# The second turn's order chosen on the chip, and half of the last layer norm run beside the last expert slots

## The chip, the cores and the metric

The kernel runs on one core of one Trainium2 chip. Its time is the device time of one execution in microseconds (us). The engines are named as the profile names them: PE is TensorE (matrix products; PEld are its weight loads), DVE is VectorE, ACT is ScalarE, POOL is GpSimd and SP is SyncE, which here issues DMA transfers and nothing else. Each engine works through its own list of instructions in order.

## The reference

Four sequences ("elements" below) of 1024 rows with 256 features pass an attention layer and then a mixture of experts. Each of the two is followed by adding its input and a layer norm without weights.

```python
x = layernorm(x + attention(x))          # 16 heads, causal, low-rank q, k, v with rotary parts
scores = (x @ router_w + router_b) / max(temperature, 0.1)
gates  = sinkhorn(scores, iters=3)       # per element: rows and columns normalised in turn
vals, idx = top_k(gates, 2)              # two experts of eight for each row
vals  = vals / (sum(vals) + 1e-8)
g = relu(x @ wg[e]);  p = x @ wp[e]      # 256 -> 512
y = (g * p) @ wo[e]                      # 512 -> 256
x = layernorm(x + sum over the two experts of vals * y)
```

4096 rows with two experts each are 8192 pairs of a row and an expert.

## The kernel before

**Attention** is computed element by element. Projections, the layer norm after attention and the router of an element are spread beside the attention of the next one by hand-written budgets (class `Lane`). After the last element's attention come its closing work, its router and the experts.

**Lists.** `route(b)` picks two experts for each row of element b. A matmul with a triangular matrix and one with ones (`so_ps`) count, for each row, how many pairs stand before it in each expert's list, and `base` carries the counts from element to element. Then `scatter` (L846) writes the element's pairs into the list `pairs` in device memory: 16 indirect DMAs, issued by POOL. Each expert owns a region of 4096 + 256 entries in that list. An entry holds the row to read, the row to add to, and the gate. `floor` (used when b is the last but one) lifts each expert's count to at least 512 before the last element is counted, so that the first 512 entries of a region hold pairs of elements 0 to 2 only, or empty ones.

**Slots.** The experts work in slots: a slot takes some consecutive entries of one expert's region.

- First turn: eight slots of 512 entries (`ER`), experts 0 to 7, the entries 0 to 511 of each region. These need nothing of the last element and begin before its router is done.
- Second turn: eight slots of 512 entries, the entries 512 to 1023. It goes through the experts in the order 7, 6, ... 0, and its first slot uses the weights of the first turn's last slot again (`like`).
- Further slots of 256 entries (`SR`), for whatever is left in any region. `lay_out` works out on the chip which expert and which entries each has. Three (`SURE`) always run, with or without entries; if more are needed, the rest run in a conditional block.

In text a slot is called by turn and place: 0_4, 1_7, 2_0. For a slot POOL gathers the rows with indirect DMAs (`gather`, L954, one for each 128 entries, into one of two `xg` buffers). PE transposes them (L993), ACT and DVE split them into a high and a low part (L190, L191), since every fp32 product is taken as three products of fp32r parts (`mm3`, L197 to L199). For each of four pieces of the 512 hidden features PE computes `gp` (gate) and `lp` (linear); ACT applies the relu (L1010), DVE multiplies (L1011), and ACT and DVE split the product (`hh`, `hl`). The output product goes to `eo`; ACT scales it by the gate (L1027) into one of six `eo` buffers, and POOL adds it to `results` in device memory with an indirect DMA that adds (L1028). `results` was filled with the rows x beforehand, so that it ends up as x plus the experts' sum. Two slots may hold the same row, so the adds of a slot wait until those of the slot before have landed (`added`, `after`). SP loads each expert's weights (three times 512 KB), ACT rounds them (L190) and DVE takes the rest (L191).

**The last layer norm** comes when all adds have landed. `results` is taken in eight chunks of 512 rows: SP loads a chunk (L1236), DVE takes mean and variance of its four row blocks (L1250, L1251), POOL works out the inverse deviation and the offset (L1253 to L1257, four small operations), ACT applies them to the first five chunks (L1260) and DVE to the last three (`DZ`, L1268), and SP stores (L1239).

**What sets the order.** The kernel is written with a tile framework: the program's order of calls gives priorities, and a scheduler arranges each engine's instructions by its own estimate of time. That order is fixed when the kernel is built. `hole` and `in_turn` and `apart` are the kernel's own helpers for the order of POOL's indirect transfers and for telling the framework which transfers can't touch the same rows. A tile pool with n buffers for a tag makes the (n+1)-th tile wait until the first one's readers are done: `xg` has two, the statistics `mv` have two, the weights' halves two.

## Time and profile before

| | us |
|---|---|
| median of 13 runs | 1055.88 (1051.23 to 1061.19) |
| profiled execution, its own time | 1054.4 |
| its span in the profile | 1052.7 |
| PE busy | 967.3 (92%) |
| DVE, ACT, POOL busy | 735.9, 624.9, 480.7 |
| first output product of an expert slot to the last output on ACT | 702.4 to 1017.9 |
| last add issued | 1021.25 |
| first load of the last layer norm issued | 1026.60 |
| mean granted clock of PE | 0.972 |

A line of a timeline has the start in us, the duration in us, the engine, the line of the program, the operation, the tile written and those read, the shapes, a count, and in brackets how long the engine stood idle before and what it waited for. `results<-eo,ents` is an indirect add of a slot, `xg<-x_rows,ents` a gather, `pairs<-ent,so_i` a scatter into the list. A line of a table by stretches has the stretch, its length, busy us and number of instructions of PE, PEld, DVE, ACT and POOL, the granted clock of PE (1.00 is full), the mean busy share of the 16 DMA engines, and GB/s. A line of the chain has the start, the duration, and what the end was waiting for then.

### The profile page before, as it was taken

The page shows a single profiled execution, that of the slowest core. Times are in us where ns is not written, and L with a number is a line of the kernel's source. Part 1 is how long each engine was busy: PE and PEld are TensorE (multiplying, and loading weights), DVE is VectorE, ACT ScalarE, POOL GpSimd, SP SyncE. Part 2 cuts the span into 40 slices and gives each one's busy share as a digit, 9 for nine tenths or more (in the row PEclk, how much of TensorE's full clock was granted, in tenths as well). Part 3 has the DMA queues.
Part 4 walks back from the last instruction along what each step waited for, and adds up shares of the span by engine and source line. Part 5 has one row for each costly group of instructions (what it writes and reads, how often), then busy time and mean ns, then how long its engine had stood idle before and what let it go on. Part 6 is the DMA issues. An engine that isn't in the chain of part 4 may idle for free.

```text
span 1052.7 us, 18000 instructions
## 1 busy us (share of the span) xinstructions
PE 967.3 (92%) x6392; PEld 605.1 (57%) x6392; DVE 735.9 (70%) x1630; ACT 624.9 (59%) x1314; POOL 480.7 (46%) x551
## 2 busy tenths in 40 slices
PE   6689999999999999999899999999999999999960
PEld 4455433455544545554345444378888888888960
DVE  3777888888888887788547898284685546555636
ACT  3544666665666666666666676755664546565633
POOL 7176521121451713354323224754477875654535
PEclk9899999999999999999999999989999999999995
DMA  6564421221422403324223330176473765655638
GB/s 242 164 214 139 115 71 56 82 76 47 132 60 67 126 2 122 111 67 122 66 75 97 88 67 3 30 250 149 101 164 94 144 143 123 174 117 137 140 53 319
DMA packets 71362, 119.66 MB, mean 114 GB/s; under 512 B 16416, under 2 KB 43040, under 8 KB 70880
## 3 DMA queue, kind: packets, MB, share of 16 engines
q1 hardware_dynamic: 48544, 81.76, 24.8%
q0 software_dynamic: 20672, 36.41, 15.9%
q8 instruction: 52, 0.85, 0.3%
q10 hardware_dynamic: 2048, 0.27, 0.2%
q14 instruction: 46, 0.38, 0.1%
HBM read 82.52 MB, written 35.60 MB: 112 GB/s over the span
## 4 chain that ended last, share of the span: by engine, by line
PE 73%; DVE 7%; DMA 7%; POOL 4%; ACT 4%; issue 3%; SPq 2%; ACTq 0%; POOLq 0%; DVEq 0%
PE y L437 12%; PE s L353 11%; PE sT L456 10%; PE gp L198 3%; PE gp L199 3%; PE gp L197 3%; PE eo L197 3%; POOL pairs L846 3%; PE eo L199 3%; PE eo L198 3%; PE s L370 2%; PE po L623 2%; PE lp L199 2%; PE lp L198 2%; PE lp L197 2%
## 5 line engine op out<-in xcount | busy, mean ns | idle before, releaser
L462 ACT ACTIVATE pT<-sT 128x512 f32<-128x512 f32 (+1 forms) x608 | 326.4, 576 | 159.1 <-PE sT L456 129.6
L374 DVE TENSOR_REDUCE mx<-s 128x1 f32<-128x384 f32 (+3 forms) x352 | 215.7, 632 | 41.2 <-PE s L370 39.9
L353 PE MATMUL s<-ks,qs 96*128 96x512 bf16 (+3 forms) x768 | 211.8, 330 | 14.5 <-DMA ks<-parts 7.1
L456 PE MATMUL sT<-qs,ks 98*128 98x512 bf16 (+3 forms) x768 | 212.4, 328 | 8.5 <-ACT pT L462 6.7
L474 POOL TENSOR_SCALAR_AFFINE_SELECT pT<-pT 128x512 f32<-128x512 f32 x120 | 75.7, 636 | 268.4 <-ACT pT L462 261.5
L383 DVE TENSOR_REDUCE mx<-s 128x1 f32<-128x512 f32 x256 | 171.2, 681 | 30.8 <-PE s L353 29.8
L437 PE MATMUL y<-pT,va 128*32 128x512 f32 (+3 forms) x1536 | 170.3, 498 | 1.0 <-POOL pT L474 0.6
L1028 POOL DMA_INDIRECT results<-eo,ents x64 | 105.4, 1647 | 81.8 <-ACT eo L1027 67.8
L353 PEld LDWEIGHTS <-qs 96*128 96x128 bf16 x768 | 71.1, 99 | 109.3 <-issue 81.8
L456 PEld LDWEIGHTS <-ks 98*128 98x128 bf16 x768 | 68.8, 99 | 94.1 <-issue 61.3
L370 PE MATMUL s<-mask,ident_b 128*128 128x128 bf16 (+2 forms) x352 | 86.8, 247 | 0.0
L1011 DVE TENSOR_TENSOR relu<-relu,lp 128x512 f32<-128x512 f32 x64 | 43.8, 684 | 61.4 <-ACT relu L1010 37.2
L191 DVE TENSOR_TENSOR wl<-w,wh 128x512 fp32r<-128x512 f32 x108 | 69.6, 684 | 22.1 <-ACT wh L190 20.6
L197 PE MATMUL eo<-wh,hh 128*128 128x256 f32 x280 | 81.6, 293 | 2.6 <-ACT eo L1027 2.1
L198 PE MATMUL eo<-wl,hh 128*128 128x256 f32 x280 | 79.3, 285 | 0.0
L954 POOL DMA_INDIRECT xg<-x_rows,ents x64 | 66.0, 1030 | 27.9 <-issue 16.1
L1010 ACT ACTIVATE relu<-gp 128x512 f32<-128x512 f32 (+1 forms) x76 | 42.7, 563 | 60.6 <-PE gp L199 60.1
L199 PE MATMUL eo<-wh,hl 128*128 128x256 f32 x280 | 78.0, 285 | 0.0
L846 POOL DMA_INDIRECT pairs<-ent,so_i x64 | 64.6, 1010 | 25.2 <-issue 17.5
L191 DVE TENSOR_TENSOR hl<-relu,hh 128x512 fp32r<-128x512 f32 (+1 forms) x76 | 48.4, 646 | 28.4 <-ACT hh L190 27.8
L437 PEld LDWEIGHTS y<-pT,va 128*32 128x32 f32 x1536 | 32.1, 108 | 62.0 <-issue 46.2
L190 ACT CAST wh<-w 128x512 fp32r<-128x512 f32 x108 | 60.7, 620 | 10.3 <-PE gp L198 7.7
(212 smaller groups left out, 1857.9 us busy)
## 6 DMA issues: line engine op xcount, KB each, us to landing
ks<-parts SPq DMA_DIRECT2D x90, 128.0 KB
w<-in_wg_dram SPq DMA_DIRECT2D x18, 512.0 KB
w<-in_wp_dram SPq DMA_DIRECT2D x18, 512.0 KB
w<-in_wo_dram SPq DMA_DIRECT2D x18, 512.0 KB
qs<-parts SPq DMA_DIRECT2D x66, 128.0 KB
parts<-lv POOLq DMA_DIRECT2D x12, 384.0 KB, 3.0
parts<-lv POOLq DMA_DIRECT2D x24, 192.0 KB, 3.2
xh<-in_x_t_dram SPq DMA_DIRECT2D x8, 512.0 KB
```

Source lines behind the costliest of these rows:

```text
L191: (sub or nc.vector).tensor_tensor(lo, src, hi.bitcast(F32), ALU.subtract)
L197: nc.tensor.matmul(ps, lhsT=sh, rhs=mh, start=(i == 0), stop=False)
L198: nc.tensor.matmul(ps, lhsT=sh, rhs=ml, start=False, stop=False)
L199: nc.tensor.matmul(ps, lhsT=sl, rhs=mh, start=False, stop=(i == n - 1))
L353: nc.tensor.matmul(ps, lhsT=q(h, half)[:NROW, t * P : (t + 1) * P], rhs=k(h, kc)[:NROW, :w], start=first, stop=last,)
L370: nc.tensor.matmul(each[:, :, w - P :], lhsT=ident_b, rhs=mask.unsqueeze(1).to_broadcast([P, m, P]), start=False, stop=True,)
L374: nc.vector.tensor_reduce(mx_of[:, half, h0 : h0 + m, t], each, AX.X, ALU.max)
L383: nc.vector.tensor_reduce(mx_of[:, kc, h, t : t + 1], ps, AX.X, ALU.max)
L437: nc.tensor.matmul(acc[g, qc][SLOT * h : SLOT * (h + 1), lo:], lhsT=va[b % 2][:, kb, at : at + SLOT], rhs=pT[:, h, lo:], start=(kb == 0), ...
L456: nc.tensor.matmul(st[:, h % m * w : (h % m + 1) * w], lhsT=k(h, kb // BPQ)[: NROW + 2, kb % BPQ * P : (kb % BPQ + 1) * P], rhs=q(h, qc)[: ...
L462: nc.scalar.activation(pT[:, h + 1 - m : h + 1, lo:], st[:, : m * w].rearrange("p (h t) -> p h t", t=w), AF.Exp, scale=scale,)
L1028: ins = nc.gpsimd.indirect_dma_start(out=results[:, :], out_offset=bass.IndirectOffsetOnAxis(ap=k.ent[:, j, 1:2], axis=0), in_=eo, in_offs ...
```

## The change

It has three parts.

1. `order_of_second`, called in the router of the second element (b = 1), takes the expert that has fewest pairs of the elements 0 and 1, and writes the order of the second turn into a table: it begins with the expert after that one and ends with it. If an expert has over 1024 pairs of these two elements, a number is added to `filled` that makes the conditional block run. The second turn's slots read their expert and their first entry from the table, as the further slots did before: SP loads the values into registers, the entries are loaded slot by slot, and no slot reuses another's weights.
2. The last second slot then holds, if its expert has at most 512 pairs of the elements 0 and 1, nothing that adds to these elements' rows, and nor does any further slot. At the beginning of that slot POOL issues four loads of 512 KB (`load_early`, after the adds of the second turn's last slot but one), which read the rows of the elements 0 and 1 from `results`. Two chunks of them are normed after that slot, one after the first further slot, one after the second (`by_scalar`: statistics on DVE, the four small operations on POOL, application on ACT, store on SP).
3. The last loop takes only the four chunks of the elements 2 and 3, the last two by DVE. In the conditional block, if it runs, the chunks of the elements 0 and 1 are normed again.

Its core ("..." marks what is left out; line numbers are not those of the profile):

```diff
-DZ = 3
+DZ = 2
...
+        if b == EARLY - 1:
+            order_of_second()
...
+    def order_of_second():
+        few = tab("few", [E])
+        nc.vector.tensor_tensor(few, floor[:1], base[:1], ALU.subtract)
+        most, again = tab("most", [1]), tab("again", [1])
+        nc.vector.tensor_reduce(most, few, AX.X, ALU.min)
+        nc.vector.tensor_scalar(again, most, -float(ER), float(NOVER), ALU.is_lt, ALU.mult)
+        tables["again"] = again
+        nc.vector.tensor_reduce(most, few, AX.X, ALU.max)
+        nc.vector.tensor_scalar(few, few, most, None, ALU.is_equal)
...
+        nc.vector.tensor_scalar(seq[:, 0], slot_no[:, :E], most, float(E + 1), ALU.subtract, ALU.add)
+        nc.vector.tensor_copy(seqi[:, 0], seq[:, 0])
+        nc.vector.tensor_single_scalar(seqi[:, 0], seqi[:, 0], E - 1, ALU.bitwise_and)
...
     def pairs_of(k):
-        if k.which == 2:
-            row = value(1, k.s, NLIST - SR)
+        if k.which:
+            row = value(k.table, 1, k.s, NLIST - k.rows)
             k.ent = const.tile([P, k.blocks, 4], I32, name=f"ent_{k.name}")
...
     def weights(k, i):
-        if k.like is not None:
-            return
-        if k.which == 2:
+        if k.which:
             if i == 0:
-                k.e = value(0, k.s, E - 1)
+                k.e = value(k.table, 0, k.s, E - 1)
...
-    def slot(k, between):
+    def slot(k, between, ahead=None):
+        if ahead is not None:
+            ahead()
...
-    second = [Slot(1, e) for e in reversed(range(E))]
-    second[0].like = first[-1]
+    second = [Slot(1, n) for n in range(E)]
...
+    def by_scalar(i, z, name):
+        rstd, off = norm_z(i, z, name)
+        for j in range(BPQ):
+            nc.scalar.activation(
+                z[:, j, :], z[:, j, :], AF.Identity, bias=off[:, j : j + 1], scale=rstd[:, j : j + 1]
+            )
+        store_z(i, z)
...
+    def load_early():
+        for i in range(n_early):
+            z = work.tile([P, T], F32, tag="yT0", name=f"ze{i}", bufs=2) if i < 2 else work.tile(
+                [P, BPQ, C], F32, tag="x1", name=f"ze{i}", bufs=X1_BUFS
+            )
+            z = early_z[i] = z.rearrange("p (n c) -> p n c", c=C) if i < 2 else z
+            ins = nc.gpsimd.dma_start(out=z, in_=rows_of(results, i))
+            for o in added:
+                after(ins, o)
+
+    def run(keys, given=(), ahead={}, behind={}):
         drain(begin(keys, 0, given))
         for n, key in enumerate(keys):
-            slot(key, begin(keys, n + 1, given))
+            slot(key, begin(keys, n + 1, given), ahead.get(n))
+            for i in behind.get(n, ()):
+                by_scalar(i, early_z[i], "e")
 
-    run(first + second + further[:SURE], (0,))
+    keys = first + second + further[:SURE]
+    n = keys.index(second[-1])
+    run(keys, (0,), {n: load_early}, {n: (0, 1), n + 1: (2,), n + 2: range(3, n_early)})
...
-    for i in range(n_z):
-        load_z(i)
-    for i in range(n_z):
+    for i in range(n_early, n_z):
+        zs[i] = zp.tile([P, BPQ, C], F32, tag="z", name=f"z{i}", bufs=n_z - n_early)
+        nc.sync.dma_start(out=zs[i], in_=rows_of(results, i))
+    for i in range(n_early, n_z):
...
         if i < n_z - DZ:
-            for j in range(BPQ):
-                nc.scalar.activation(
-                    z[:, j, :], z[:, j, :], AF.Identity, bias=off[:, j : j + 1], scale=rstd[:, j : j + 1]
-                )
-            store_z(i, z)
+            by_scalar(i, zs[i], "f")
         else:
-            rest.append((i, z, rstd, off))
+            rest.append((i, zs[i], *norm_z(i, zs[i], "f")))
```

`norm_z` holds the statistics and POOL's four operations as the old loop had them. In the second turn's order as built, places are written 1_0 to 1_7; which expert stands at a place is known only on the chip.

## Prediction

> **What bounds the kernel now.** I read first the chain that ended last, then the busy time by stretches, then POOL's, ACT's, DVE's and SP's timelines at the two places that the change touches. The chain's shares:
>
> ```profile
> PE 73%; DVE 7%; DMA 7%; POOL 4%; ACT 4%; issue 3%; SPq 2%; ACTq 0%; POOLq 0%; DVEq 0%
> ```
>
> So TensorE sets the time, and where it doesn't (the end), DMA and DVE do. By stretches (busy us and instructions of each engine, granted clock, DMA share, GB/s):
>
> ```profile
> 800.00:860.00 60.00, 58.27 (x349) 51.14 (x348) 32.36 (x52) 33.23 (x65) 48.49 (x38) 1.00 0.59 124
> 980.00:1000.00 20.00, 19.30 (x149) 18.33 (x148) 13.10 (x26) 13.28 (x32) 10.17 (x7) 1.00 0.60 134
> 1000.00:1020.00 20.00, 16.79 (x139) 16.39 (x137) 8.25 (x20) 9.63 (x25) 7.28 (x5) 1.00 0.34 55
> 1020.00:1040.00 20.00, 0.00 (x0) 0.00 (x0) 9.52 (x48) 6.01 (x12) 9.61 (x20) 0.55 0.75 257
> ```
>
> The reader is to see that PE is all but full up to the last slots, that POOL is the second busiest engine where the turns meet (48.49 of 60), and that from 1020 on PE does nothing: the final layer norm stands alone there. Where the turns meet, POOL's queue:
>
> ```profile
> 791.50 1.00 POOL L846 DMA_INDIRECT pairs<-ent,so_i  x1 [0.30 <-DVE upto L877]
> ...
> 812.32 1.10 POOL L846 DMA_INDIRECT pairs<-ent,so_i  x1 [0.30 <-issue]
> 813.72 1.61 POOL L1028 DMA_INDIRECT results<-eo,ents  x1 [0.31 <-issue]
> 821.22 1.05 POOL L954 DMA_INDIRECT xg<-x_rows,ents  x1 [0.30 <-PE gp L198]
> 825.27 1.43 POOL L954 DMA_INDIRECT xg<-x_rows,ents  x1 [0.30 <-issue]
> ```
>
> Sixteen scatters of the last element's pairs take 791.50 to 813.72; then come four adds, and the gathers of the first second slot (821.22 to 826.7). PE transposes what they bring at 838.18, 7 to 11 us after it lands. The price of the delayed adds shows on ACT, and on PE behind it (the only two PE rows that I take from there):
>
> ```profile
> 817.65 0.47 ACT L1027 ACTIVATE eo<-eo,ents 128x256 f32<-128x256 f32 x1 [5.00 <-DMA results<-eo,ents]
> ...
> 818.17 0.38 PE L197 MATMUL eo<-wh,hh 128*128 128x256 f32 x1 [1.49 <-ACT eo L1027]
> ...
> 838.18 0.60 PE L993 MATMUL xgT_ps<-ident,xg 128*128 128x128 f32 x4
> ```
>
> At the end:
>
> ```profile
> 980.48 1.56 POOL L1028 DMA_INDIRECT results<-eo,ents  x1 [1.01 <-ACT eo L1027]
> 1005.13 0.38 ACT L1010 ACTIVATE relu<-gp 128x256 f32<-128x256 f32 x1 [0.38 <-PE gp L199]
> 1017.40 0.47 ACT L1027 ACTIVATE eo<-eo,ent 128x256 f32<-128x256 f32 x1 [1.78 <-PE eo L199]
> 1014.82 3.82 DMA results<-eo,ent
> 1019.40 6.56 DMA results<-eo,ent
> 1026.60 3.77 SPq L1236 DMA_DIRECT2D z<-results  x8
> 1038.46 1.37 DVE L1250 BATCH_NORM_STATS2 bnst_f<-z 128x6 f32<-128x256 f32 x4
> 1047.31 0.23 POOL L1257 TENSOR_SCALAR off_f<-off_f 128x4 f32<-128x4 f32 x1
> 1047.58 1.38 DVE L1268 TENSOR_SCALAR z<-z,rstd_f,off_f 128x256 f32<-128x256 f32 x4 [0.67 <-POOL off_f L1257]
> ```
>
> An add issued at 1014.82 lands at 1018.64 and POOL's next waiting instruction starts at 1019.40: 4.58 from add to dependent add. From the first z load to the span's end are 1052.7 − 1026.60 = 26.1 us.
>
> **The change, part by part.** Times are of the profiled run, whose own time is 1054.4 (span 1052.7, 1.7 around it); the median is 1055.88, so I add 1.5 at the end.
>
> *Final loop, four chunks instead of eight.* POOL's four little operations a chunk (1.9 us) set the pace. The eighth chunk's last ends at 1047.54; the fourth's would end at 1039.53 with no fifth between. That is 8.0 less; the 1.38 us of DVE, the store and the end behind it stay. Bounds: 4 × 1.57 (DVE's pitch of a chunk, 1036.90 to 1038.46) = 6.3, and 4 × 2.08 (ACT's four norms of a chunk) = 8.3. **−8.0**.
>
> *Adds after the last output.* Before, last ACT scale ends at 1017.87 and the loads go at 1026.60: 8.7. In the built order the last slot's two outputs come as one piece of 24 matmuls, during which the slot's before lands, so only their own adds are left; the least is one add's pitch 1.87 and the row's 3.8 + 1.6 to the load, 7.0. **−1.7** (between −1.7 and 0).
>
> *(a) Where the turns meet.* The order of POOL changes (PE's matmuls that count the lists move too, from 787 to 796.5): after the first turn's last gathers come two adds of the slot then on PE, and only then the sixteen scatters. The second add waits for ACT's scale, which ended at 798.6, so the scatters start at 800.6 instead of 791.50. Sixteen take 22.2 (to 822.8). Then two adds (1.87 each); the next slot's first add waits for their landing: 824.7 + 4.58 = 829.3; four adds to 836.7; then the gathers, four by 1.28, the last issued at 840.6. A gather lands 2.8 to 5.8 us after issue in this trace: 843.4 to 846.4. PE wants the blocks at 838.18. It stands 5.2 to 8.2; the four land one by one, so I take the lower end: **+5.2**. The eo stall of 2.1 us in before (1.49 and the transposes' lateness) is gone, but the gather, not PE's arrival, now decides, so that gains nothing; if gathers came in time, it would give −2.1, which is the lower bound.
>
> *(b) Early norms in the 256-row slots.* The first early load waits for the adds of the last slot but one. Its last add was issued at 980.48; with (a) at 985.7; the built order puts twelve 512-wide matmuls (0.23 us each, 2.8) ahead of its last product: 988.5. Add to dependent 4.58: 993.1. The third of the final loop's loads landed at 1033.64, 7.0 after the first's issue, and issues are about 0.5 to 0.85 apart (0.85 on POOL, rows of x_rows<-x, which landed in 4.3 median): the first lands at 997.4, the fourth about 8.4 after the start, 1001.5. On **DVE** the first statistics stand ahead of the first small slot's first relu product, so all relu work waits for 997.4 + 1.4. From there to the second small slot's first product DVE has four products and four splits (0.41 each), six weight splits (0.63), two xl (0.42), three chunks of statistics (1.57): 12.6. That makes 1011.4. On **POOL** the four adds of the last second slot wait for the early loads (they write what those read): 1002.3 to 1009.8; behind them the second chunk's chain, mixed with the third's, 3.3: 1013.1. On **ACT** the second chunk's norm waits for that, and the third's and fourth's stand behind it, ahead of the second small slot's third and fourth relu: three by 1.55 and 1.4 of its own work, so that the fourth relu comes at 1019.4. In before it was 1005.13, with (a) 1010.3: 9.1 late. After that point the built order leaves PE twelve 256-wide matmuls more than before (0.12 each): 1.4. **+10.5.** Bounds: if POOL's chain came ahead of the adds, only DVE's order would hold (12.6 against 11.84 between the same two products in before, and the first 3 us): about +3; if each further chunk waits for its buffer too (statistics buffers are two) and the loads share with weights at twice the time (+8.4): +18.
>
> *At nothing:* the first second slot now loads its own expert's weights, six ACT casts (0.62) and six DVE subtractions (0.68): ACT and DVE have 33.23 and 32.36 of 60 there; without that cover 4 us. Three 512 KB loads more on SP, which has only loads to issue; the register loads ahead of them delay each by about a microsecond against a slot of 17.9 us of PE. One 32 KB list per slot instead of a common one lands a slot ahead. Thirteen tiny DVE operations for the order run beside the second element's attention; 13 × 0.4 = 5 us if PE waited for them. The four early stores are on SP behind everything that a slot needs.
>
> **Sum:** −8.0 − 1.7 + 5.2 + 10.5 = +6.0. 1054.4 + 6.0 + 1.5 = **1061.9**.
>
> *A rule against it.* The row at 817.65 shows ACT standing 5.00 us for a buffer, with a cast (818.02) and a relu (818.53) behind it that had their inputs. The Trainium skill, "PSUM — Partial Sum Buffer", section Engine vs sequencer instructions, says that the queues of ScalarE, VectorE and GpSimdE are strict FIFO. By it, (b) is paid in full; by the averages of the stretches alone (DVE 13.10, ACT 13.28 of 20) it would be nothing and the sum −4.5. The page "Perfetto Trace Analysis", section Optimization Strategy, speaks for the change: interleaving regimes with different bounds may help.
>
> *Clock.* After an idle 7.1 us early in the trace (41.5 to 48.5) the granted clock is 0.50 for 4 us; after the 1.49 us at 816.7 it stays 1.00. The stall of (a) lies between; in four pieces it is nearer the second, so 0, with +2 at the other end. The page "TensorE: Matmul & The Clock Gate", section What's actually happening, puts the limit at about 3.4 us idle, by which one unbroken stall would pay the 2.
>
> **Rivals.**
> 1. *The norms do hide* (ends faster). DVE and ACT have 7 us of 20 free; if the early loads land before the small slots' relu (that is, by 993), (b) is 1 and the sum −9.7 + 5.2 + 1 = −3.5: 1052.4. It decides from the point where (b) is below 4.5. Against: 980.48 + 4.58 + 4.3 = 989.4 already in before's order, against the product at 988.48.
> 2. *Neither stall:* −9.7 + 0.5: 1046.7. For it: PE's counting matmuls may run as early as before, and the scatters with them. Against: the scatters' 22.2 us on a POOL at 48.49 of 60.
> 3. *Only (b):* the gathers come in time, −9.7 − 2.1 + 10.5 = −1.3 to −9.7 + 10.5 = +0.8: 1054.6 to 1056.7.
> 4. *Transfers collide:* 2 MB read and 2 MB written beside weights where DMA is at 0.60, with a cold clock: (b) 18, (a) 7: +15.3, 1071.2.
> 5. *It doesn't do what it says:* if the chosen expert had over 512 pairs of the first two elements, spare slots would run in addition. The reference's router on these inputs gives 472 to 598, the smallest expert 472, and the further slots needed are three, those that always run; so no.
>
> **How the numbers follow.** Chances: forecast 0.62 (its own range 1057.5 to 1068), rival 1 0.13, 2 0.05, 3 0.08, 4 0.11, 5 0.01. A measurement of this kernel tells 0.2%, 2.1 us. Faster: rivals 1 and 2, 0.18. Same: most of 3, 0.07. Slower: the forecast, 4 and 5, 0.75. Leaving out rival 2 and the far half of 4 gives 1051.5 to 1071.
>
> **What would show it.** Right: gathers of the first second slot issued after 835 and PE idle about 5 us before its transposes; DVE idle before the first early statistics with "DMA ze"; PE busy well under 16 of 20 in the stretches of the small slots; z loads to end about 18 us. Wrong: PE full through the small slots (rival 1), or early loads landing far from 4 to 8 us after issue.

## The result and the profile after

The changed kernel takes **1078.06 us** (median of 10 runs, 1075.31 to 1081.46) against 1055.51 for the kernel before (46 runs): a ratio of 1.0214, 95% interval 1.0198 to 1.0230, or 22.5 us more. The forecast was 1061.9 with a range to 1071.0: the sign was right, the size was not. The profiled execution of after has a span of 1074.4, 21.7 more than the 1052.7 of before, and a time of its own of 1076.1. Six of the eighteen runs below were made, like these, on chips on which the kernel before takes 1056 to 1058 us; the others on chips on which it takes 1102 to 1107 us for another reason (see the last section), so each is told as a ratio to the kernel before on its own chip.

The shares of the chain that ended last, in after:

```profile
PE 70%; DMA 9%; DVE 7%; ACT 5%; POOL 4%; issue 3%; SPq 2%; ACTq 0%; POOLq 0%; DVEq 0%
```

PE has lost 3 points; DMA has 2 more and ACT one. The same stretches as before, in after (busy us and instructions of PE, PEld, DVE, ACT, POOL, then granted clock, DMA share, GB/s):

```profile
800.00:860.00 60.00, 52.64 (x297) 45.22 (x296) 31.43 (x65) 30.42 (x60) 43.76 (x35) 0.94 0.51 115
...
1000.00:1020.00 20.00, 12.98 (x86) 12.37 (x85) 12.27 (x42) 9.70 (x23) 12.05 (x14) 0.83 0.74 238
1020.00:1040.00 20.00, 14.02 (x95) 13.07 (x95) 7.08 (x22) 12.44 (x30) 9.38 (x15) 0.83 0.46 112
1040.00:1060.00 20.00, 6.76 (x51) 5.99 (x49) 3.27 (x9) 3.30 (x8) 6.15 (x4) 0.81 0.41 87
```

PE is no longer full in two places: where the turns meet (52.64 of 60, it was 58.27) and in the small slots (12.98 and 14.02 of 20). In both the granted clock is below 1; in before it was 1.00 in the same stretches up to 1020. No other engine is full over 20 us: DVE and ACT never pass 12.5 of 20 in the small slots. So no engine became the bound; what is missing is time in which the engines wait for each other and for transfers.

To see how much each place costs I lay the two traces' PE lists side by side: PE does the same matmuls in both, so for a moment of before I count the output columns done by then and look up when after has done as many. The difference of the two times is PE's *lag*. What it grows by between two points is what that part of the program lost.

| part | forecast | measured |
|---|---|---|
| to 838 (attention, first turn) | 0 | +0.5 |
| (a) where the turns meet (to 842) | +5.2 | +9.6 |
| second turn (860 to 990) | 0 | +1.4 |
| (b) small slots (990 to 1017) | +10.5 | +18.9 |
| last scale on ACT to the z loads: 7.10, was 8.73 | −1.7 | −1.6 |
| z loads to the end: 18.83, was 26.1 | −8.0 | −7.3 |
| sum | +6.0 | +21.7 |

The rows add up to 21.5; with the lag at the last ACT scale (1048.47 against 1017.87, 30.6) in place of the first four it is 21.7. Both gains came, to 0.1 and 0.7 us. Both losses came in the places named, at nearly twice the size each.

**Where the turns meet.** The timeline of after, POOL's indirect transfers and what PE waited for behind them:

```profile
800.52 1.57 POOL L1052 DMA_INDIRECT results<-eo,ents  x1 [4.24 <-ACT eo L1051]
802.40 1.48 POOL L850 DMA_INDIRECT pairs<-ent,so_i  x1 [0.30 <-issue]
...
825.61 1.60 POOL L1052 DMA_INDIRECT results<-eo,ents  x1 [0.30 <-ACT hh L192]
827.51 1.56 POOL L1052 DMA_INDIRECT results<-eo,ents  x1 [0.30 <-issue]
832.20 1.77 POOL L1052 DMA_INDIRECT results<-eo,ents  x1 [3.13 <-ACT hh L192]
...
839.84 1.00 POOL L981 DMA_INDIRECT xg<-x_rows,ent  x1 [0.30 <-issue]
...
843.68 0.95 POOL L981 DMA_INDIRECT xg<-x_rows,ent  x1 [0.30 <-issue]
842.76 0.30 PE L1015 MATMUL xgT_ps<-ident,xg 128*128 128x128 f32 x1 [3.87 <-DMA xg<-x_rows,ent]
843.95 0.34 PE L1015 MATMUL xgT_ps<-ident,xg 128*128 128x128 f32 x1 [0.90 <-DMA xg<-x_rows,ent]
846.43 0.80 PE L1015 MATMUL xgT_ps<-ident,xg 128*128 128x128 f32 x2 [2.15 <-DMA xg<-x_rows,ent]
```

The reader is to see the forecast order link by link: the second add held back the scatters to 802.40 (in before they began at 791.50), the scatters held back the adds, the add at 827.51 had to land before that at 832.20 (the profile names an ACT cast for this wait; that it was the landing is read from the program, where a slot's adds wait for those of the slot before, and from the distance of 4.69, for 4.58 in before), and the gathers that stood last in the queue went out at 839.84 to 843.68 instead of 821.22 to 825.27. PE stood 3.87, 0.90 and 2.15 us, 6.92 in all. The two stretches of 4 us behind it:

```profile
844.00:848.00 4.00, 1.85 (x8) 1.51 (x9) 0.11 (x1) 0.73 (x2) 3.08 (x4) 0.52 0.40 114
848.00:852.00 4.00, 4.00 (x19) 3.52 (x19) 2.93 (x5) 2.90 (x6) 3.30 (x3) 0.63 0.27 85
```

After the stand the granted clock was 0.52 and then 0.63. Busy time times what is missing of the clock is 1.85 × 0.48 + 4.00 × 0.37 = 2.4 us. 6.9 and 2.4 are the 9.6 but for 0.3.

**The small slots.** The chain of work that ended last in after, where it passes the small slots:

```profile
995.00 8.30 DMA results<-eo,ent
...
1003.91 3.72 DMA ze<-results
1007.65 1.40 DVE bnst_e L1249 x4
```

The same add in POOL's timeline:

```profile
995.00 3.28 POOL L1052 DMA_INDIRECT results<-eo,ent  x1 [1.26 <-ACT eo L1051]
```

The last add of the last slot but one took 8.30 us to land; the median of all adds is 3.9 in both traces, though single ones of before took up to 7.7. Two things came together at it: POOL itself was at this add for 3.28 us, where the median is 1.57, and SP issued three weight loads of 512 KB behind it (996.90, 998.64, 999.20). Only when it had landed could POOL issue the early loads, and the first chunk's statistics, which stand ahead of the slot's relu products on DVE, began at 1007.65. The timeline of after, what waited for that and for POOL's little operations:

```profile
1007.65 1.40 DVE L1249 BATCH_NORM_STATS2 bnst_e<-ze 128x6 f32<-128x256 f32 x4 [10.45 <-DMA ze<-results]
1009.56 0.58 PE L199 MATMUL gp<-xh,wh 128*128 128x256 f32 x1 [4.68 <-DVE relu L1035]
1013.44 1.69 POOL L1052 DMA_INDIRECT results<-eo,ent  x1 [0.94 <-ACT wh L192]
1019.74 1.55 POOL L1052 DMA_INDIRECT results<-eo,ent  x1 [0.30 <-issue]
...
1024.45 2.08 ACT L1262 ACTIVATE ze<-ze,off_e,rstd_e 128x256 f32<-128x256 f32 x4 [3.61 <-POOL off_e L1256]
...
1029.23 2.06 ACT L1262 ACTIVATE ze<-ze,off_e,rstd_e 128x256 f32<-128x256 f32 x4
1029.84 0.58 PE L199 MATMUL gp<-xh,wh 128*128 128x256 f32 x1 [2.11 <-DVE relu L1035]
```

DVE stood 10.45 us for the first early load, and PE 4.68 for DVE. The four adds at 1013.44 to 1019.74 put the second chunk's chain behind them, so ACT stood 3.61 us and then gave 6.2 us to three norms, with the relus that PE needed between and behind them. This is the order that the forecast gave. The granted clock in that stretch:

```profile
1008.00:1012.00 4.00, 2.44 (x11) 2.44 (x12) 3.92 (x16) 2.42 (x6) 2.89 (x6) 0.50 0.86 315
1012.00:1016.00 4.00, 3.59 (x20) 3.38 (x18) 4.00 (x13) 4.00 (x10) 2.75 (x3) 0.65 0.15 36
...
1028.00:1032.00 4.00, 1.30 (x4) 1.01 (x5) 0.47 (x2) 4.00 (x11) 0.06 (x1) 0.56 0.51 202
1032.00:1036.00 4.00, 4.00 (x22) 4.00 (x22) 2.35 (x7) 2.79 (x8) 2.16 (x2) 0.59 0.61 168
```

By the same sum, 2.44 × 0.50 + 3.59 × 0.35 + 1.30 × 0.44 + 4.00 × 0.41 = 4.7 us of PE's work were lost to the clock; in before it was 1.00 up to 1020. What that costs in time is less certain. Behind the second pair of stretches (2.2) PE runs without a gap up to 1044, so there it counts; behind the first pair (2.5) PE soon stands for DVE and ACT again, and a slower PE may only have filled such waits.

### The profile page after: what moved, and what is told of

It reads as the page before. It is cut to its first block, busy times and chain, and to the rows that moved or that the text cites. A ratio compares the mean times of both kernels' runs of the same rounds, so it can differ in the third digit from the quotient of the medians.

```text
span 1074.4 us, 18122 instructions
## 1 busy us (share of the span) xinstructions
PE 975.7 (91%) x6392; PEld 608.0 (57%) x6392; DVE 739.5 (69%) x1646; ACT 629.9 (59%) x1324; POOL 485.0 (45%) x555
## 4 chain that ended last, share of the span: by engine, by line
PE 70%; DMA 9%; DVE 7%; ACT 5%; POOL 4%; issue 3%; SPq 2%; ACTq 0%; POOLq 0%; DVEq 0%
PE y L439 12%; PE s L355 11%; PE sT L458 10%; DMA results<-eo,ent 3%; PE gp L200 3%; PE gp L201 3%; PE eo L199 3%; PE lp L200 3%; PE lp L201 3%; PE gp L199 3%; PE lp L199 3%; PE eo L201 3%; PE eo L200 3%; PE po L625 2%; PE s L372 2%
## 5 line engine op out<-in xcount | busy, mean ns | idle before, releaser
L193 DVE TENSOR_TENSOR wl<-w,wh 128x512 fp32r<-128x512 f32 x114 | 74.3, 686 | 23.3 <-ACT wh L192 23.1
L1052 POOL DMA_INDIRECT results<-eo,ent x38 | 65.1, 1714 | 48.1 <-ACT eo L1051 23.2
L850 POOL DMA_INDIRECT pairs<-ent,so_i x64 | 65.6, 1024 | 24.9 <-issue 17.5
L199 PE MATMUL gp<-xh,wh 128*128 128x512 f32 (+1 forms) x176 | 65.9, 383 | 10.2 <-DVE relu L1035 8.1
L1052 POOL DMA_INDIRECT results<-eo,ents x32 | 51.4, 1606 | 51.9 <-ACT eo L1051 37.1
L192 ACT CAST wh<-w 128x512 fp32r<-128x512 f32 x114 | 64.0, 618 | 7.1 <-PE gp L200 4.8
L200 PE MATMUL gp<-xl,wh 128*128 128x512 f32 (+1 forms) x176 | 66.7, 380 | 1.1 <-DVE xl L193 1.1
```

The costliest lines, as they stand in the source:

```text
L199: nc.tensor.matmul(ps, lhsT=sh, rhs=mh, start=(i == 0), stop=False)
L200: nc.tensor.matmul(ps, lhsT=sh, rhs=ml, start=False, stop=False)
L1052: ins = nc.gpsimd.indirect_dma_start(out=results[:, :], out_offset=bass.IndirectOffsetOnAxis(ap=k.ent[:, j, 1:2], axis=0), in_=eo, in_offs ...
```

## The experiments

The theory after the result (A): (a) is POOL's order, (b) is the early norms standing in strict queues behind transfers that come late, and the cold clock adds to both. Rivals: (B) the small slots have no room for the norms, wherever they stand; (C) the collision of transfers is the cause, and without it the norms would hide; (D) the two statistics buffers hold DVE up. Four measures are used in the table: the growth of PE's lag against the trace of before from 838 to 860 (a) and from 860 to 1017 (b, with the 1 us of drift between), and the two parts of the end. Against the same trace the kernel before itself, run again, grows by 0.0 and 0.1.

| run | ratio, 95% interval | 838–860 | 860–1017 | last scale to z loads (before 8.73) | z loads to end (before 26.1) |
|---|---|---|---|---|---|
| the change | 1.0214, 1.0198–1.0230 | 9.8 | 20.3 | 7.1 | 18.8 |
| h0 the kernel before | 0.9993, 0.9974–1.0012 | 0.0 | 0.1 | 9.2 | 25.8 |
| h1 norms' statistics after the slots, table's order | 1.0135, 1.0086–1.0184 | 9.3 | 9.0 | 8.6 | 20.8 |
| h2 the same, fixed order | 1.0002, 0.9981–1.0022 | 0.1 | 0.7 | 12.6 | 21.3 |
| h3 four statistics buffers | 1.0194, 1.0153–1.0234 | 10.6 | 20.6 | 7.3 | 18.2 |
| i1 spaced statistics, fixed order | 1.0056, 1.0033–1.0078 | 0.1 | 14.7 | 7.2 | 18.3 |
| i2 spaced, table's order, entries first | 1.0078, 1.0050–1.0105 | 5.2 | 15.0 | 8.9 | 18.0 |
| *chips at 1102 to 1107:* | | | | | |
| g0 the change | 1.0059, 1.0031–1.0087 | 6.6 | 21.3 | 7.0 | 18.9 |
| e1 / f1 order alone | 0.9952, 0.9930–0.9974 / 0.9928, 0.9896–0.9959 | 5.1 / 4.0 | 3.9 / 3.2 | 7.7 / 6.8 | 26.8 / 26.7 |
| e2 norms alone | 1.0056, 1.0032–1.0080 | (18 before 838) 0.0 | 14.5 | 10.6 | 18.4 |
| e3 / f3 / g1 norms after the last scale | 1.0044, 1.0015–1.0073 / 1.0048, 1.0026–1.0071 / 1.0056, 1.0030–1.0083 | 1.6 / 7.0 / 7.2 | 3.0 / 3.6 / 7.6 | 24.7 / 24.6 / 21.5 | 18.9 / 19.6 / 18.8 |
| e4 / f4 entries first | 1.0049, 1.0019–1.0078 / 1.0085, 1.0065–1.0105 | (15 to 16 before 838) 0.6 / 0.6 | 19.5 / 19.8 | 7.4 / 7.2 | 18.8 / 19.9 |
| f5 / g2 both | 1.0088, 1.0071–1.0104 / 1.0112, 1.0061–1.0164 | (16 before 838) 0.6 / 0.6 | 3.8 / 3.2 | 24.5 / 24.4 | 19.0 / 18.9 |
| g3 two weight sets reused | 1.0030, 1.0005–1.0055 | 6.2 | 16.0 | 9.9 | 19.2 |

### One part alone: the order (e1, f1), the norms (e2)

e1 and f1 keep the order from the table and leave out the early norms:

```diff
-DZ = 2
+DZ = 3
-    run(keys, (0,), {n: load_early}, {n: (0, 1), n + 1: (2,), n + 2: range(3, n_early)})
+    run(keys, (0,))
...
-    for i in range(n_early, n_z):
+    for i in range(n_z):
```

> Part 1 of the change alone: the second turn's order from the table, entries and weights loaded slot by slot; no early norm, the last loop takes all eight chunks, three of them on DVE. Theory A (two separate stalls, and a shorter last loop): the stall where the turns meet stays whole, +9.6 as read from the changed kernel's trace (PE 0.5 us late at 838, 10.2 at 842), and nothing else, so about 1065 (1064 to 1067). Theory B (the stall comes from the early norms, through the scheduler's order, or the dynamic slots cost something at each slot): 1056 to 1058 in the first case, over 1070 in the second.

> The kernel of the run that has part 1 alone, once more, since the chip of the first four runs took 1101.58 us for the kernel before (against 1055.51) and stood still for 11 us where the turns meet, with nothing in the profile that it waited for. Expected where the kernel before takes about 1055: theory A (the late gather is a consequence of the table-driven order alone) +9 to +11; theory B (it needs the early norms too) 0 to +2. Where the kernel before takes about 1101 again: the same ratio as then, 0.993 to 0.997.

e2 keeps the norms and returns to an order written in the program:

```diff
-        if b == EARLY - 1:
-            order_of_second()
...
-    second = [Slot(1, n) for n in range(E)]
+    second = [Slot(1, e) for e in (7, 6, 5, 4, 3, 2, 0, 1)]
+    second[0].like = first[-1]
```

> Part 2 alone: the second turn in a fixed order 7, 6, 5, 4, 3, 2, 0, 1 (expert 1 has the fewest pairs of the first two elements with these inputs, so the result is the same), its first slot with the weights of the slot before, entries in one load; early loads and early norms as in the change. Theory A: no stall where the turns meet; the early norms cost what they cost in the changed kernel, 18.9 between 990 and 1017 of the old time, less what the built order spares (here the second chunk's chain stands on POOL ahead of three of the four adds): 8 to 19, against 8.9 gained at the end: -1 to +10, 1055 to 1066. Theory B (most of the 18.9 is a consequence of the late gather): 1047 to 1050.

The first clause of e1's text missed: the time is 1097.82, on a chip where the kernel before takes 1101.58, and the order alone is 0.5 to 0.7% *faster* there (f1's text for this case, 0.993 to 0.997, is met but for the last digit, 0.9928). e2's profile shows why. With the order of before, the scatters stand alone in POOL's queue, and on these chips everything else stands with them (lines of e2's timeline and one stretch):

```profile
817.35 1.00 POOL L848 DMA_INDIRECT pairs<-ent,so_i  x1 [0.30 <-DVE upto L902]
...
836.47 0.96 POOL L848 DMA_INDIRECT pairs<-ent,so_i  x1 [0.30 <-issue]
836.81 0.84 ACT L1055 ACTIVATE eo<-eo,ents 128x256 f32<-128x256 f32 x2 [12.32 <-remote]
837.33 1.11 PE L1019 MATMUL xgT_ps<-ident,xg 128*128 128x128 f32 x4 [11.35 <-issue]
```

```profile
830.00:835.00 5.00, 0.00 (x0) 0.00 (x0) 0.00 (x0) 0.00 (x0) 3.84 (x4) 0.50 0.03 2
```

PE loses 18 us there in the order of before (lag 25.1 at 800, 43.2 at 838). With the table's order it loses 13.2 in e1, 11.5 in f1 and 14.1 in g0 (800 to 860), presumably since part of the scatters' time and of the late gathers' is the same time. So on these chips (a) is hidden behind a stall of their own, and these runs don't measure it. They do measure (b): 14.5 in e2, whose end gains 26.1 − 18.4 = 7.7, and which is slower by 0.56%; 21.3 in g0, the change itself there (its ratio is only 1.0059 since its (a) is a gain there):

> The changed kernel itself, as the measure for the other runs beside it, since two chips so far took 1101.6 and 1107.0 us for the kernel before. Where that takes about 1055: +22.5 as measured, 1078. Where it takes about 1100 or more: on these chips part 1 alone gained 5 to 8 us and the norms in the gap lost 5, so if the early norms cost 10 to 19 as theory A has it, +12 to +25; if the slow chips hide them (theory B), +5 or less.

The 6.5 us (0.59% of 1107; 4.9 between the medians) are less than theory A's text had, which took (a) for a loss there too, and lie at the edge of theory B's band; but B's ground, that these chips hide the early norms, is not what the trace shows, with (b) at 21.3.

### The statistics behind the last slot (e3, f3, g1; with the entries first f5, g2)

The norms' place is taken out of the small slots: their statistics wait for ACT's last scale. f3 and g1 are the same kernel on other chips; f5 and g2 add the edit of e4, below.

```diff
-            nc.vector.bn_stats(st, z[:, j, :])
+            ins = nc.vector.bn_stats(st, z[:, j, :])
+            if name == "e":
+                after(ins, scaled[0])
...
-    run(keys, (0,), {n: load_early}, {n: (0, 1), n + 1: (2,), n + 2: range(3, n_early)})
+    run(keys, (0,), {n: load_early}, {len(keys) - 1: range(n_early)})
```

> The changed kernel with the early chunks loaded as before, but their statistics made to wait for the last ACT scale of the last slot, so that the four early norms run in the gap between the last output and the first load of the last loop. Theory A (the 18.9 us come from the norms' place in the queues of DVE, ACT and POOL): they go, the end keeps its gain, the stall where the turns meet stays: +9.6 - 8.9 + 0 to 3, so 1056 to 1060. Theory B (the early loads themselves, which the adds of the last second slot wait for and which share DMA with weights, cost it): 10 or more of the 18.9 stay, 1067 or more.

> The changed kernel with the early norms in the gap behind the last output, once more. Where the kernel before takes about 1055: theory A (the norms' place in the queues costs the 18.9 us) +1 to +4; theory B (the early loads cost it) +11 or more.

> The changed kernel with the early norms in the gap behind the last output. Against the changed kernel beside it: theory A (the norms' place in the queues) 16 to 20 us faster, theory B (the early loads) within 8 us of it.

> Both edits together: norms in the gap, entries first. Theory A (two separate stalls, and a gain of 8.9 at the end): -9 to -6 against the kernel before, about 1047 to 1050 where that takes 1055. Theory B (the stalls come from loads that stay in): +5 or more.

> Norms in the gap and the first second slot's entries first. Where the kernel before takes about 1055: theory A (two stalls, both gone, the end 8.9 shorter) 1047 to 1050; theory B +5 or more. Where it takes about 1100: as in the run of this kind before, +8 to +11.

In the time, theory A's gains did not come: f3, f5 and g2 are slower than the kernel before by 0.5 to 1.1%, and g1 is level with the change beside it, as theory B's text had it; only e3 (3.7 us between the medians) is inside A's 1056 to 1060 when that is read as a difference. The mechanism came: (b) falls from 21.3 to between 3.0 and 7.6. What was freed is lost again behind it. The lines of e3's timeline:

```profile
1064.18 1.54 POOL L1052 DMA_INDIRECT results<-eo,ent  x1 [0.30 <-issue]
1069.91 6.46 SPq L1242 DMA_DIRECT2D out_dram<-ze  x4
1083.34 1.75 SPq L1313 DMA_DIRECT2D z<-results  x4
```

The last add was issued at 1064.18, and the last loop's loads went at 1083.34, 19.2 later; in before that distance was 1026.60 − 1021.25 = 5.4. Between the two stand the four stores of the early chunks, in front of the loads on SP. From the last scale to the loads it takes 21.5 to 24.7 instead of 7.0. That the loads wait for the stores is read from their order and the distance; h1, with the stores behind the loads, has 8.6. A wait moved out of the small slots became a new one ahead of the end, of nearly the same size.

### The entries and the gathers first (e4, f4)

```diff
+            if nxt is second[0] and i == 1:
+                pairs_of(nxt)
...
-            pairs_of(k)
+            if k.ent is None:
+                pairs_of(k)
```

SP loads the first second slot's entries ahead of the third weight load, and POOL's gathers of it come ahead of the adds.

> The changed kernel with one load moved: the entries of the first second slot are asked for on SP ahead of that slot's third weight load, and the built order then puts its gathers ahead of the adds of slot 0_5. Theory A (the gathers come late because they stand behind four adds on POOL): they go at about 831 and land by 838, the stall shrinks from 9.6 to 0 to 2, so 1068 to 1071. Theory B (the entries themselves land late, because SP has the third weight load and the register loads ahead of them, or the scatters end at 825): gathers after 835, the stall stays over 5, 1074 or more.

> The changed kernel with the first second slot's entries asked for ahead of its third weight load, gathers ahead of the adds of slot 0_5, once more. Where the kernel before takes about 1055: theory A (four adds on POOL hold the gathers) +12 to +15 against +22.5 of the change; theory B (the entries land late anyway) +20 or more.

f4 is the same kernel on another chip. Both texts missed. On these chips the gathers' place changes nothing that can be seen: PE stands earlier, with the scatters, and no longer at the gathers (0.6 from 838 to 860, 15 to 16 from 800 to 838). The question was left for a chip without that stall (i2 below).

### The weight loads beside the adds (g3)

The second and third small slot reuse the raw weights of the first, so that two thirds of the loads beside the late add are gone (these two slots then work with a wrong expert's weights, and the output isn't the reference's).

```diff
+        if k.which == 2 and k.s in (1, 2):
+            k.raw[i] = further[0].raw[i]
+            return
```

> The changed kernel without the weight transfers of the further slots 2_1 and 2_2 (six of 512 KB): these slots split the weights of 2_0 again, so that ACT, DVE and PE have the same work; the output is that of the wrong expert there. In the changed kernel the last add of the last slot but one took 8.3 us to land (3.8 is usual) while three weight loads ran at 273 GB/s, and the early loads waited for it. Theory A (the weights delayed that add, and through it DVE and PE): the add lands in about 3.8, PE's wait of 4.7 for the first relu product shrinks to about 0.5, and with the clock staying up 5 to 8 us are gained against the changed kernel. Theory B (the add is late for another reason): within 2 us of it.

In g3 the early loads go 6.2 us after the last add (1038.17 − 1031.95), in g0 9.0 (1038.39 − 1029.37), and the first early statistics begin 9.8 after it instead of 12.9 (1041.79 and 1042.28); (b) falls from 21.3 to 16.0, but the loads of the last loop came 2.85 later behind the last scale. The edit also changed the built order: in g3 the next small slot's gathers (1035.54, 1036.85) stand ahead of the early loads, which then wait for nothing that the profile names, so 6.2 is only an upper bound for the landing, and a part of the gain in (b) may be the gathers'. In the time, 1.0030 and 1.0059 have intervals that overlap, with medians 2.0 us apart, so theory A's 5 to 8 did not come. The weight transfers cost some 3 us up to the statistics, and 16 of the 21 us of (b) are there with two thirds of them gone: rival C is a part of the cause and not the whole.

Which of the transfers is late hardly matters to the norms. In e4 the same add, with the same weight loads behind it, held POOL for 2.07 us (e4's timeline):

```profile
1028.30 2.07 POOL L1053 DMA_INDIRECT results<-eo,ent  x1 [1.27 <-ACT eo L1052]
1033.97 2.24 POOL L1281 DMA_DIRECT2D ze<-results  x4 [3.60 <-DMA results<-eo,ent]
1040.51 1.41 DVE L1253 BATCH_NORM_STATS2 bnst_e<-ze 128x6 f32<-128x256 f32 x4 [10.02 <-DMA ze<-results]
```

The loads went after 5.67 us, but the first one then took 6.54 to be there, instead of 3.74 in after. From the add to the statistics it is 12.2, for 12.65 in after, and (b) is 19.5; f4, the same kernel with 3.28 us on POOL and 8.96 to the loads, has 19.8. Over all runs with the table's order and early loads, this add holds POOL for 2.07 to 2.09 us (e3, e4, f3, f5, g2; 5.6 to 5.8 to the loads) or for 3.28 (the change, f4, g0, g1, h1, h3, i2; 8.8 to 9.2, and g3); with the fixed order it is 1.55 (e2, h2, i1; 4.6 to 5.2). Why POOL is at it so long no run shows.

### Statistics behind the slots, stores behind the loads (h0, h1, h2), and buffers (h3)

h0 is the kernel before, unchanged, as a measure of the method. h1 puts the statistics and POOL's operations behind the last split of the last small slot, and the application and the stores of the early chunks behind the last loop's loads, with statistics buffers of their own; the renewal of the early chunks in the conditional block is left out.

```diff
+            if name == "e":
+                after(ins, halved[0])
...
-    run(keys, (0,), {n: load_early}, {n: (0, 1), n + 1: (2,), n + 2: range(3, n_early)})
+    run(keys, (0,), {n: load_early}, {len(keys) - 1: ()})
+    normed = [norm_z(i, early_z[i], "e") for i in range(n_early)]
...
+    for i in range(n_early):
+        by_scalar(i, early_z[i], "e")
```

h2 is h1 with e2's fixed order. h3 gives the early chunks' `mv` four buffers instead of two and changes nothing else.

> The kernel before, with a profile, on a chip like those of the experiments. Theory A (the experiments' chips hold all engines but POOL during a burst of scatters, and the kernel before loses more at the burst where the turns meet than the changed kernel does): PE loses about 18 us between 800 and 845, as in the run with the norms alone, which has the same order there, against 14 to 15 in the changed kernel beside its 9.6. Theory B (these chips are slower evenly): PE's lag grows evenly, and under 5 us there.

> The changed kernel with the early chunks' statistics and POOL's operations in the gap behind the last slot, and their application and stores after the conditional block, ahead of the last four chunks (the renewal of the early chunks inside the block is left out; the block doesn't run). In the run with the norms in the gap, PE ended 13 to 17 us earlier than in the changed kernel, but the last loop's loads went at 1083.34, 14 us after the last add had landed, since SP had the early stores ahead of them. Theory A (the stores ahead of the loads ate the gain): the loads go within 6 us of the last landing, and 8 to 13 us are gained against the run with the norms in the gap: 0.990 to 0.996 of the kernel before. Theory B (something else holds the loads): 1.000 or more.

> The same placing of the early norms with the second turn in the fixed order 7, 6, 5, 4, 3, 2, 0, 1, entries in one load and the weights of the slot before used again. Theory A: where the turns meet as the kernel before, so -9 to -5 us: 0.991 to 0.996 of it on any chip. Theory B (the stall of the norms comes back, or the loads stay late): 1.000 or more.

> The changed kernel with four buffers instead of two for the early chunks' statistics, so that the fourth chunk's means on DVE no longer wait for POOL's offset of the second, which stands behind the four adds. Theory A (this wait is one of the links that hold the second small slot's relu on DVE; ACT's norms still wait for POOL): 1 to 4 us gained against the changed kernel. Theory B (it is hidden behind ACT): 0 to 1.

These four ran on a chip without the stall (1057.76 for the kernel before), which the texts of h0 and h1 had not counted on. h1 and h2 missed theory A's 0.990 to 0.996, and h2's text had said "on any chip". h0 is 0.9993: the measures repeat, but for 3 us of drift in attention (see the last section). h3 is the change, to within its interval, and its lag is no less (20.6 for 20.3): rival D is out.

h2 shows the mechanism most plainly: with the fixed order and no norm between the slots, PE's list runs as in before through both places (0.1 and 0.7), with the early loads still there. h1 has (a) in full, 9.3, and keeps 9.0 of (b), with no norm in the small slots. Its timeline says which:

```profile
996.16 3.28 POOL L1056 DMA_INDIRECT results<-eo,ent  x1 [1.26 <-ACT eo L1055]
1005.36 2.24 POOL L1283 DMA_DIRECT2D ze<-results  x4 [5.92 <-DMA results<-eo,ent]
1008.67 1.25 POOL L985 DMA_INDIRECT xg<-x_rows,ent  x1 [1.07 <-PE xgT_ps L1019]
1015.54 0.45 PE L1019 MATMUL xgT_ps<-ident,xg 128*128 128x128 f32 x1 [2.63 <-DMA xg<-x_rows,ent]
```

The early loads themselves hold POOL: they wait 5.92 us for the late add, the next small slot's gathers stand behind them, and PE waits for those. So of (b) in the change some 9 stay without the norms, the loads' place on POOL among them, and about 11 (20.3 − 9.0) go with the norms' place on DVE, POOL and ACT. What stays depends on how late that add is: it is 7.6 in g1 and 9.0 in h1, where the loads go 8.8 and 9.2 after it, and 3.0 to 3.8 in e3, f3, f5 and g2, where they go 5.6 to 5.8 after it. In h2 the same loads waited too, but went at 988.07, 4.58 after the add at 983.49, with the gathers at 991.50 in time.

The time of h2 is that of before, so the gain at the end was not won either: from the last scale to the end it is 34.8 in before, 25.9 in the change and 33.8 in h2. The lines of h2's timeline:

```profile
1025.64 1.56 POOL L1060 DMA_INDIRECT results<-eo,ent  x1 [0.17 <-issue]
1033.41 1.77 SPq L1316 DMA_DIRECT2D z<-results  x4
1035.23 5.97 SPq L1251 DMA_DIRECT2D out_dram<-ze  x4
1041.82 1.41 DVE L1258 BATCH_NORM_STATS2 bnst_f<-z 128x6 f32<-128x256 f32 x4 [1.72 <-DMA z<-results]
```

The last add went 4.39 us later than in before (1025.64 against 1021.25; 3.0 of that is h2's lag) and the loads 12.6 after the last scale instead of 8.7; then the early stores ran beside the loads, and the third chunk of z was there only at 1041.82, 8.4 after the issue of the loads. Loads to end are 21.3 instead of 18.8. The early norms' work was moved from the slots to the end, and there it costs what it saved.

### Spacing the statistics (i1), and the gathers first on a chip without the stall (i2)

The statistics of chunks 0 and 1 stand behind the last split of the first small slot, those of 2 and 3 behind splits of the second, each with buffers of its own; the application and stores follow in the slots. i1 has the fixed order, i2 the table's order with the entries and gathers first. The renewal in the conditional block is left out in both.

```diff
-            nc.vector.bn_stats(st, z[:, j, :])
+            ins = nc.vector.bn_stats(st, z[:, j, :])
+            if name == "e":
+                after(ins, split_last[(("2_0", 3), ("2_0", 3), ("2_1", 1), ("2_1", 3))[i]])
...
-    run(keys, (0,), {n: load_early}, {n: (0, 1), n + 1: (2,), n + 2: range(3, n_early)})
+    run(keys, (0,), {n: load_early}, {n + 1: (0, 1), n + 2: (2, 3)})
```

> The experts' order is fixed (7, 6, 5, 4, 3, 2, 0, 1) and the first second slot shares the weights of the slot before it, so (a) is gone as in h2. The statistics of early chunks 0 and 1 stand on DVE behind the last split of the first small slot, those of chunks 2 and 3 behind splits of the second one, each with buffers of its own; the application and the stores follow inside the small slots, so the end is not held up by them as in h2. Left out: the renewal of early chunks under the condition. Theory A ((b) is only the loads' lateness on DVE's and POOL's queues): (b) 0 to 4, end as in the change (-9.7 + up to 3), so 0.993 to 0.999 of the kernel before. Rival B (DVE and ACT have no room in the small slots wherever the norms stand): (b) 8 or more, 1.000 to 1.008.

> The same spacing of the statistics, with the table's order of the change, and with the load of the first second slot's entries ahead of the third weight load and the four gathers ahead of the adds of the slot on PE. Theory A ((a) is POOL's order, gathers behind the adds): (a) 2 to 5, so 2 to 5 us over the run with the fixed order. Rival B ((a) is the scatters, which the table holds back, and the gathers' place is of no use): 8 to 10 us over it.

i1 is 1.0056, with (b) at 14.7. Theory A's 0 to 4 missed, and both numbers lie in rival B's band, but its trace doesn't show B's mechanism. The early loads landed in time and DVE waited for none, so rival C alone is out as well. The lines of i1's timeline:

```profile
1009.38 1.65 POOL L1058 DMA_INDIRECT results<-eo,ent  x1 [1.20 <-DMA results<-eo,ents]
...
1013.38 0.23 POOL L1265 TENSOR_SCALAR off_e<-off_e 128x4 f32<-128x4 f32 x1
1013.65 2.07 ACT L1271 ACTIVATE ze<-ze,off_e,rstd_e 128x256 f32<-128x256 f32 x4 [6.60 <-POOL off_e L1265]
1016.03 0.58 PE L201 MATMUL gp<-xh,wh 128*128 128x256 f32 x1 [7.26 <-ACT xh L194]
```

The first chunk's four little POOL operations are split by two adds, the first of which (1009.38) has to wait for an earlier add's landing; ACT's norm waits 6.60 us for them, and the cast (`xh`) that PE needs stands behind that norm. PE stands 7.26 us, with the clock at 0.50 after it. ACT was idle for those 6.60 us: there was room, and the queue's order used it up. The end of i1 is as good as that of the change (7.2 and 18.3), so its 14.7 of lag are what keeps it from being faster.

i2 shows (a) at 5.2 instead of 9.3 to 10.6. The gathers went at 832.18 to 836.45 and no transpose waited for them; what PE waits for instead is ACT, which stands 3.43 us for an eo buffer whose adds now come behind the gathers (i2's timeline):

```profile
836.45 0.95 POOL L984 DMA_INDIRECT xg<-x_rows,ent  x1 [0.30 <-issue]
837.70 1.77 POOL L1055 DMA_INDIRECT results<-eo,ents  x1 [0.30 <-issue]
842.83 0.47 ACT L1054 ACTIVATE eo<-eo,ents 128x256 f32<-128x256 f32 x1 [3.43 <-DMA results<-eo,ents]
```

So theory A for (a) holds, about at the ends of its 2 to 5 (5.2 by lag, 2.1 between the medians; i2's profiled run is the slowest of its four, 1070.06 against a median of 1065.96): some half of (a) is the gathers' place. The other half is read from these lines and not tested by a run of its own: what isn't late at the gathers is late at the adds, behind the same scatters.

No version was found that beats the kernel before on a chip where it takes 1056 us; h2, with 1.0002, comes nearest.

## Why the prediction was wrong, and where it was right

The places and the mechanisms were right. What failed are sizes: the path from the last add to the first early statistics, the norms on ACT, the start and length of the scatters, and *Clock*, which was taken as nothing.

- *Final loop*, −8.0: right, −7.3 (18.83 against 26.1).
- *Adds after the last output*, −1.7: right, −1.6 (7.10 against 8.73).
- *(a) Where the turns meet*, +5.2: the mechanism was right and the size was not, 9.6. The second add's time was met (800.52 for 800.6). Two terms were short: I let the scatters begin when that add is issued, not one pitch later (1.8), and gave them 22.2 where they took 825.61 − 802.40 = 23.2; these two are 2.8 of the 3.1 by which the gathers came late (839.84 for 836.7), and PE stood 6.92 instead of 5.2. (The gathers' slack in before, told as 7 to 11 us, is 7 to 14: the first landed at 824.07, the last at 831.06.) And *Clock* was taken as 0 on the ground that four pieces of a stall are nearer to the short one; measured, the pieces (3.87, 0.90, 2.15) brought it to 0.52 and cost 2.4.
- *(b) Early norms in the 256-row slots*, +10.5: the mechanism was right, DVE, POOL and ACT each at the named instruction, and the size was not, 18.9. Up to the second small slot's fourth relu the forecast had 9.1; it came at 1031.82, which against 1005.13 and the 11.7 by which PE was late already at 990 is 15.0. Of these 5.9, 3.8 are there when the first statistics begin. The step that failed is the path "Add to dependent 4.58" and "the first lands" 4.3 later: the 4.58 came from the end of before, where no weight loads ran beside the add, and the 8.9 of the two were 12.65 here (1007.65 − 995.00). In after it is the add that was late (8.91 to the loads, which then took 3.74); in e4 the loads themselves. Another 1.1 is there when the second chunk's norm begins on ACT, and 1.1 more come with the three norms, which the text took at 1.55 each beside a row of before with 2.08; they took 2.06 to 2.08. (The text's terms add up to 1019.2, not 1019.4.) Behind the fourth relu the forecast had 1.4 and 3.9 were lost. Here *Clock* is missing, which was weighed for (a) and left out of (b): 2.2 in the stretches from 1028 to 1036. The place of the loads on POOL, ahead of the small slot's gathers, which the forecast didn't price at all, is the wait that h1 shows in its 9.0, where the norms are away; in the change DVE's wait covers it.
- The bound of +18 for (b) rested on statistics buffers and on loads shared with weights. The buffers gave nothing (h3). The sharing was real, though in after it struck the add ahead of the loads and not the loads.
- *Rival 4*, transfers collide with a cold clock ((b) 18, (a) 7: 1071.2), was the nearest, with 0.11; it was 0.9 short in (b) and 2.6 in (a). *Rival 1*, that the norms hide, and *rival 2* are ruled out by the change, and rival 1 by i1 as well. *Rival 3*, only (b), is ruled out since (a) was there. *Rival 5*: after has 38 adds of the kind `results<-eo,ent`, 8 slots of 4 and 3 of 2, so no spare slot ran.
- *At nothing*: the lag at 838 is 0.5, which shows no cost of the thirteen little operations beside attention, but only to the 3.1 us that the kernel before, run again, differs by there (h0). Over the second turn the lag grows by 1.4 (0.1 in h0), which is what the weight loads and the lists can have cost.
- The Trainium skill, "PSUM — Partial Sum Buffer", section Engine vs sequencer instructions, has the queues of ScalarE, VectorE and GpSimdE as strict FIFO. The runs agree: in i1 ACT was idle for 6.60 us with a norm at its head, and the cast that PE waited for stood behind that norm.
- The page "TensorE: Matmul & The Clock Gate", section What's actually happening, puts the limit at about 3.4 us idle. In after the clock was 0.52 behind a stand of 3.87 and 0.50 behind one of 4.68, and stayed 1.00 behind 1.49 in before, all of which agree. It was also 0.56 from 1028 on, behind stands of 1.74 and 2.11 with 0.4 of work between them, each below the limit: here pieces did count together. In the forecast I set the rule aside for a guess about pieces; the first piece of (a) alone was over it.

## What to carry to other kernels

Work that is moved beside a busy engine is not paid in busy time but in the order of the queues: before moving it, name for each queue what its first instruction waits for and what stands behind that, the DMA queues' landing times included, and take the landing time from a row with the same traffic beside it. Where a stall of PE is near 4 us, its price can include the clock after it (here 2.4 of 9.6, and some 2.2 of 18.9 behind two shorter ones). And a gain at the end of a kernel is only kept if the moved work's stores don't stand ahead of the last loads: in e3, with the stores ahead of them, the loads came some 16 us later than in before (24.7 behind the last scale, for 8.7). With the stores behind the loads the rest of the moved work still cost what it saved: in h2 9 us of gain became one.

## What the runs showed of the hardware that was not expected

- **The last indirect add before the early loads held POOL for 1.55, 2.07 or 3.28 us, by the run.** With 3.28 and weight loads behind it, it landed in 8.30 us (median of all adds 3.9) and its dependent came 8.8 to 9.2 after it; with 2.07 and the same loads 5.6 to 5.8; with 1.55, in the fixed order, 4.6 to 5.2. Without two of the three weight sets (g3) the dependent came after 6.2 in spite of 3.28 on POOL. Why its time on POOL differs stays open.
- **On some chips all engines but POOL stand during a burst of scatters.** There the kernel before takes 1102 to 1107 us instead of 1056. In e2 nothing ran on PE, DVE or ACT from 830 to 835 while POOL issued a scatter every 1.26 us, and the DMA engines moved 2 GB/s. PE's lag against the trace of before grows by 18 to 23 between 555 and 690 us, in attention (3.2 in h0), and by 18 more in e2 between 800 and 838. The profile names no semaphore for it ("issue", "remote"). Its cause is not settled here.
- **So a change can have another sign on another chip.** Part (a) costs PE 9 to 11 us where the engines don't stand, and the order alone is 0.5 to 0.7% faster where they do; the whole change is 1.0214 on the one and 1.0059 on the other.
